# The recurrent stage of a four-block kernel: query sum in PSUM, gate inputs of 64 steps in a bank, exp sums by copies, one gate op per half

## The chip, the cores and the metric

The kernel runs on one core of one Trainium2 chip. A core has five engines that run their own instruction streams and meet through semaphores: TensorE (PE; weight loads are listed apart as PEld), VectorE (DVE), ScalarE (ACT), GpSimd (POOL) and SyncE (SP), which issues the DMAs. Matmuls write PSUM, whose banks hold 512 float32 values in each of 128 partitions. The metric is the device time of one execution in microseconds.

## The reference

A sequence `x` (2 batches, 512 positions, 128 channels) passes through four blocks, L0 to L3. Each adds two parts to it, a conditioned one (`xcond`) and a feed-forward one (`ffn`), each on a layer norm of `x`. All is float32. The change touches L1's `xcond` alone. That part is a recurrent cell (GRU) of 512 steps, which at each step attends over the 77 context vectors of its batch with the state as query:

```
def step(h, x_t):
    hid = broadcast(h[:, None, :], (B, 77, 128))
    combined = concatenate([hid, enc_hiddens], axis=2)
    score = tanh(einsum('bsk,kh->bsh', combined, W_att))
    score = einsum('bsh,h->bs', score, V_att[:, 0])
    attn = softmax(score, axis=-1)
    context = einsum('bs,bsh->bh', attn, enc_hiddens)
    inp = concatenate([x_t, context], axis=1)
    gz, gr, gh = split(inp @ Wi + b, 3, axis=1)
    rz, rr, rh = split(h @ Uh, 3, axis=1)
    z = sigmoid(gz + rz)
    r = sigmoid(gr + rr)
    hh = tanh(gh + r * rh)
    h_new = z * h + (1.0 - z) * hh
    return h_new, h_new
outs = scan(step, last_hidden, x_t of 512 positions)
```

`B` is 2, `h` has 128 channels, and `last_hidden` is the conditioning vector. No step can begin before the state of the step before it is there.

## The kernel before

The function `tile_kernel` runs eight phases one after the other, two for each block. Tensors are kept with 128 positions or 128 channels on the partitions. Weights come by DMA three phases ahead. The phase that matters is `l1_xcond` (lines 571 to 663). It keeps channels on the partitions, so that the state `h` of a step is a tile of 128 x 2, one column per batch, in `hs[:, s, :]`.

Ahead of the loop it prepares what does not depend on the state. `gx` holds for each of 512 positions eight columns: the input's share of the three gates for two batches (with the bias), and two columns of zeros. `stat` (128 x 2 x 77) is the context's share of the argument of the score's tanh. `gc` (128 x 2 x 3 x 77) is the product of each context vector with the three gates' weights, so that the context vector itself is never formed. `vrep` holds the score vector in all of its 128 columns: a matmul with it leaves the scores on every partition. `uhh` is half of the last third of `Uh`, since the sigmoids are computed as tanh of half the argument.

A step of the loop then does this, one line of the profile for each operation (matmuls go through the helper at line 222, and are told apart by the tiles that they write and read: `mm`, `tr` and `o` are PSUM tiles, of three, three and two banks):

- The query: `pu` (mm) is a matmul of `wtop` with `h`. L621, on VectorE and for each batch, adds its column to that batch's 77 columns of `stat` and writes `x`. L623 is the tanh on ScalarE (`th`). The matmul with `vrep` (tr) gives the scores.
- The state's share of the gates: a bank `pc` (o) holds eight columns. It was filled during the step before with `gx` of this step, by a matmul with the identity (`gates_in`). Three more matmuls add the state's share (`uh` twice, `uhh` once with `h` read twice), the first of them between the query and the scores, the others behind the scores.
- The softmax and the context's share: L631 takes the negated largest score of each batch (`nm`). L636 takes the exponential on ScalarE (`e`), and with `accum_out` its sum (`se`), which a second instruction reads out of an accumulator. L637 multiplies `gc` by `e` (`pr`, 231 columns per batch). L639 inverts the sums (`ri`), L641 reduces both batches of `pr` to six columns (`pre`), L642 multiplies them by `ri`, and L643 adds the six columns of `pc`.
- The gates: L645 is the tanh of the first two gates of both batches (`zr`). L648, one per batch, is the tanh of the candidate (`hh`), with its bias and scale read from `pre` and `zr`. L651, L653 and L654 form the two factors of the blend, and L656, one per batch, writes the new state's column into `hs`.

The loop stands inside `manual_schedule()`: each engine issues its instructions of the loop in the order in which the program states them. Which semaphores an instruction waits for is worked out by the framework from the tiles that it reads and writes.

Every float32 matmul here shows as two passes, each with a weight load and a matmul of its own, so a step has 14 of each.

## Time and profile before

| | us |
|---|---|
| median of 3 runs | 6283.16 (6280.9 to 6301.28) |
| the profiled execution's own time | 6284.0 |
| its span, first to last instruction | 6282.2 |
| PE, PEld, DVE, ACT, POOL busy | 4528.6, 3080.0, 3299.4, 2077.1, 227.0 |
| the loop of 512 steps | 258.6 to 3281.2 |
| mean granted TensorE clock | 0.665 |

Times are microseconds from the start of the span. An engine's busy time is that of its own instructions, without waits. A line of the costliest groups reads: source line, engine, operation, tiles written and read, shapes, count, then busy time, mean duration in ns, and idle time of the engine just ahead of the group with what ended most of it. The granted clock is the share of TensorE's full speed that it was given. The slices below cut the span in 40 equal parts, some 157 us each; a digit is the busy share (or the clock) in tenths:

```
PE   4855555555555555555559999798888888888888
DVE  6555555555555555555555443453636353545423
ACT  1333333333333333333333333132323232333322
PEclk7855555555555555555559998787969697878856
```

### The profile page before, as it was taken

Reading aid. Unit: us, or ns where it says so; the run is one execution under the profiler, and the core shown is the slowest. Engines: PE = TensorE matmul, PEld = TensorE weight load, DVE = VectorE, ACT = ScalarE, POOL = GpSimd, SP = SyncE. Lnnn points to the kernel's source line nnn. Section 1 sums busy time; section 2 is a strip of 40 time slices with the busy share of each in tenths; the row PEclk is TensorE's granted clock in tenths of the full one; section 3 lists DMA queues with packets and bytes.
Section 4 is the critical chain, followed back from the end, with each engine's and each line's share of the span. In section 5 each row is a group of like instructions: output and inputs, shape, how many; then the busy total and the mean of one; then the engine's idle time right before and its main releaser. Section 6 shows DMA issues by size and latency. Waiting matters only on the chain. (4 is left out here: it accounts for less than half of the span.)

```text
span 6282.2 us, 63201 instructions
## 1 busy us (share of the span) xinstructions
PE 4528.6 (72%) x21576; PEld 3080.0 (49%) x21576; DVE 3299.4 (53%) x10933; ACT 2077.1 (33%) x6069; POOL 227.0 (4%) x228
## 2 busy tenths in 40 slices
PE   4855555555555555555559999798888888888888
PEld 2655555555555555555555667534333333333356
DVE  6555555555555555555555443453636353545423
ACT  1333333333333333333333333132323232333322
POOL 2000000000000000000000000100000010101000
PEclk7855555555555555555559998787969697878856
DMA  1000000000000000000000000100000000000000
GB/s 37 26 1 1 0 1 1 1 1 1 1 1 1 1 1 1 1 1 1 1 15 21 1 1 4 37 1 2 10 1 12 1 12 1 13 1 1 1 0 4
DMA packets 6973, 32.96 MB, mean 5 GB/s; under 512 B 1872, under 2 KB 4202, under 8 KB 4986
## 3 DMA queue, kind: packets, MB, share of 16 engines
q1 hardware_dynamic: 6650, 28.93, 1.3%
q8 instruction: 170, 2.79, 0.2%
q14 instruction: 153, 1.25, 0.1%
HBM read 28.40 MB, written 0.52 MB: 5 GB/s over the span
## 5 line engine op out<-in xcount | busy, mean ns | idle before, releaser
L222 PE MATMUL mm<-hs,w1x 128*128 128x2 f32 x1024 | 300.2, 363 | 1203.8 <-DVE hs L656 1203.8
L222 PEld LDWEIGHTS mm<-hs,w1x 128*128 128x128 f32 x1024 | 256.2, 310 | 1252.1 <-DVE hs L656 1249.0
L1058 DVE TENSOR_REDUCE peak<-st 128x2 f32<-128x1024 f32 (+1 forms) x480 | 528.8, 1136 | 311.1 <-PE st L222 306.0
L222 PE MATMUL tr<-th,vrep 128*128 128x77 f32 x2048 | 580.5, 436 | 120.5 <-ACT th L623 120.5
L222 PE MATMUL st<-qx,km 32*128 32x512 f32 (+1 forms) x1920 | 533.1, 717 | 69.3 <-DVE peak L1058 62.5
L222 PEld LDWEIGHTS o<-hs,w1x 128*128 128x128 f32 x2048 | 559.3, 333 | 0.0
L222 PEld LDWEIGHTS tr<-th,vrep 128*128 128x128 f32 x2048 | 473.7, 321 | 164.5 <-ACT th L623 164.5
L222 PE MATMUL o<-hs,w1x 128*128 128x2 f32 x2048 | 549.7, 338 | 0.0
L631 DVE TENSOR_REDUCE nm<-tr 128x1 f32<-128x77 f32 x1024 | 243.4, 238 | 570.7 <-PE tr L222 570.7
L1159 ACT ACTIVATE pT<-st 128x1024 f32<-128x1024 f32 x384 | 388.5, 1023 | 430.2 <-PE st L222 429.4
L636 ACT ACTIVATE e<-tr,nm 128x77 f32<-128x77 f32 x1024 | 334.1, 326 | 463.9 <-DVE nm L631 458.0
L623 ACT ACTIVATE th<-x 128x77 f32<-128x77 f32 x1024 | 226.7, 268 | 654.3 <-DVE x L621 654.3
L222 PE MATMUL st<-km,qm 32*128 32x512 f32 (+1 forms) x3072 | 410.7, 541 | 41.5 <-DVE qm L1043 16.6
L637 DVE TENSOR_TENSOR pr<-gc,e 128x231 f32<-128x231 f32 x1024 | 409.7, 400 | 43.0 <-ACT e L636 0.8
L621 DVE TENSOR_SCALAR x<-stat,mm 128x77 f32<-128x77 f32 x1024 | 226.4, 264 | 358.9 <-PE mm L222 358.9
L645 ACT ACTIVATE zr<-pre 128x4 f32<-128x4 f32 x512 | 105.5, 206 | 823.3 <-DVE pre L643 823.3
L641 DVE TENSOR_REDUCE pre<-pr 128x6 f32<-128x462 f32 x512 | 324.7, 634 | 0.0
L222 PEld LDWEIGHTS st<-km,qm 32*128 32x128 f32 x3072 | 206.4, 247 | 212.5 <-issue 89.4
L648 ACT ACTIVATE hh<-o,pre,zr 128x1 f32<-128x1 f32 x1024 | 303.8, 347 | 17.8 <-ACT zr L645 0.2
L222 PEld LDWEIGHTS st<-qx,km 32*128 32x128 f32 (+1 forms) x1920 | 150.7, 192 | 319.4 <-DVE peak L1058 201.6
L222 PE MATMUL o<-gx,ident 128*128 128x8 f32 x1024 | 293.8, 361 | 0.0
L222 PE MATMUL o<-hs,uhh 128*128 128x4 f32 x1024 | 290.5, 354 | 0.0
(340 smaller groups left out, 6621.8 us busy)
## 6 DMA issues: line engine op xcount, KB each, us to landing
w3x<-in_w3x SPq DMA_DIRECT2D x6, 1664.0 KB, 7.3
w1g<-in_w1g SPq DMA_DIRECT2D x1, 2560.0 KB, 9.0
w2a<-in_w2a SPq DMA_DIRECT2D x1, 2176.0 KB, 8.5
w2b<-in_w2b SPq DMA_DIRECT2D x1, 2176.0 KB, 9.0
w3f<-in_w3f SPq DMA_DIRECT2D x1, 1940.0 KB
w0g<-in_w0g SPq DMA_DIRECT2D x1, 1760.0 KB, 12.7
w1d<-in_w1d SPq DMA_DIRECT2D x1, 1288.0 KB, 5.5
rows<-in_rows SPq DMA_DIRECT2D x1, 1108.5 KB, 8.4
```

What stands on the lines that cost most here:

```text
L222: pe.matmul(o, lhsT, rhs, start=start, stop=stop)
L621: dve.tensor_scalar(x, stat[:, b, :], pu[:, b : b + 1], None, ALU.add)
L623: act.activation(th, x, AF.Tanh)
L631: dve.reduce_max(nm[:, b : b + 1], pb[b], axis=AX.X, negate=True)
L636: act.activation(e[:, b, :], pb[b], AF.Exp, bias=nm[:, b : b + 1], accum_out=se[:, b : b + 1])
L637: dve.tensor_tensor(pr[:, b], gc[:, b], bcast(e[:, b, :], [P, 3, NC], 1), ALU.mult)
L641: dve.tensor_reduce(pre, pr, AX.X, ALU.add)
L645: act.activation(zr, pre[:, :, 0:2], AF.Tanh, scale=0.5)
L648: act.activation(hh[:, b : b + 1], pc[:, 6 + b : 7 + b], AF.Tanh, bias=pre[:, b, 2:3], scale=zr[:, b, 1:2])
L1058: dve.tensor_reduce(dst if dst.ndim == 2 else dst.rearrange("p t r -> p r t"), src, AX.X, ALU.max, negate=True)
L1159: act.activation(pT[:, 2 * p : 2 * p + 2, :], ps, AF.Exp)
```

## The change

All of it lies in `l1_xcond`.

- The sum of query and context is formed in PSUM. `states_in` fills 154 columns of a bank with `stat`, by a matmul with the identity, ahead of the step that uses it. In the step, one matmul per batch adds `wtop` times the state, with the batch's column of `h` read 77 times over (a stride-0 operand). The tanh reads PSUM. The two operations of L621 are gone.
- `gates_in` fills a whole bank, 512 columns, with `gx` of 64 steps at once. A step uses its eight columns of that bank. The first of the three matmuls that add the state's share moves behind the scores, to the two others.
- The exponential no longer sums. A copy of `e` on ScalarE, one per batch and behind both exponentials, has the `accum_out` instead.
- The reduction of `pr` stands ahead of the reciprocal and writes a tile of its own, `cg`. The product with `ri` and the sum with `pc` become one operation per batch.

```diff
+            SB = 64
             gx = r1.tile([P, S, 4, B], F32, tag="gx", name="gx")
...
             def gates_in(s):
 
-                pc = o_tile()[:, :8]
-                mm(pc, ident, gx[:, s].rearrange("p g b -> p (g b)"), start=True, stop=False)
-                return pc
+                bank = o_tile()
+                mm(bank, ident, gx[:, s : s + SB].rearrange("p s g b -> p (s g b)"))
+                return bank
+
+            def states_in():
+
+                xp = mm_tile()[:, :n2].rearrange("p (b n) -> p b n", b=B)
+                mm(xp, ident, stat)
+                return xp
+
+            def add(o, lhsT, rhs):
+                pe.matmul(o, lhsT, rhs, start=False, stop=True, skip_group_check=True)
 
             with tc.manual_schedule():
-                pc = gates_in(0)
+                bank, xp = gates_in(0), states_in()
                 for s in range(S):
                     h = hs[:, s, :]
-                    pu = mm_tile()[:, :B]
-                    mm(pu, w("wtop"), h)
-                    mm(pc[:, 0:2], w("uh")[:, :P], h, start=False, stop=False)
+                    pc = bank[:, 8 * (s % SB) : 8 * (s % SB) + 8]
                     pb = []
                     for b in range(B):
-                        x = rs.tile([P, NC], F32, tag="x", name="x")
-                        dve.tensor_scalar(x, stat[:, b, :], pu[:, b : b + 1], None, ALU.add)
+                        add(xp[:, b, :], w("wtop"), h[:, b : b + 1].to_broadcast([P, NC]))
+                    for b in range(B):
                         th = rs.tile([P, NC], F32, tag="th", name="th")
-                        act.activation(th, x, AF.Tanh)
+                        act.activation(th, xp[:, b, :], AF.Tanh)
                         t = tr_tile()[:, :NC]
                         mm(t, vrep, th)
                         pb.append(t)
-                    mm(pc[:, 2:4], w("uh")[:, P : 2 * P], h, start=False, stop=False)
-                    mm(pc[:, 4:8].rearrange("p (c b) -> p c b", b=B), uhh, bcast(h, [P, 2, B], 1), start=False, stop=True)
+                    for g in range(2):
+                        add(pc[:, 2 * g : 2 * g + 2], w("uh")[:, g * P : (g + 1) * P], h)
+                    add(pc[:, 4:8].rearrange("p (c b) -> p c b", b=B), uhh, bcast(h, [P, 2, B], 1))
+                    if s + 1 < S:
+                        xp = states_in()
...
                     for b in range(B):
-                        act.activation(e[:, b, :], pb[b], AF.Exp, bias=nm[:, b : b + 1], accum_out=se[:, b : b + 1])
+                        act.activation(e[:, b, :], pb[b], AF.Exp, bias=nm[:, b : b + 1])
                         dve.tensor_tensor(pr[:, b], gc[:, b], bcast(e[:, b, :], [P, 3, NC], 1), ALU.mult)
+                    for b in range(B):
+                        es = rs.tile([P, NC], F32, tag="es", name="es")
+                        act.activation(es, e[:, b, :], AF.Copy, accum_out=se[:, b : b + 1])
+                    cg = rs.tile([P, B, 3], F32, tag="cg", name="cg")
+                    dve.tensor_reduce(cg, pr, AX.X, ALU.add)
                     ri = rs.tile([P, B], F32, tag="ri", name="ri")
                     dve.reciprocal(ri, se)
                     pre = rs.tile([P, B, 3], F32, tag="pre", name="pre")
-                    dve.tensor_reduce(pre, pr, AX.X, ALU.add)
-                    dve.tensor_tensor(pre, pre, bcast(ri, [P, B, 3], 2), ALU.mult)
-                    dve.tensor_tensor(pre, pc[:, 0:6].rearrange("p (g b) -> p b g", b=B), pre, ALU.add)
+                    for b in range(B):
+                        dve.scalar_tensor_tensor(pre[:, b, :], cg[:, b, :], ri[:, b : b + 1], pc[:, b : 6 : B], ALU.mult, ALU.add)
...
-                    pcn = gates_in(s + 1) if s + 1 < S else None
+                    if (s + 1) % SB == 0 and s + 1 < S:
+                        bank = gates_in(s + 1)
...
-                    pc = pcn
```

## The prediction

> **What bounds it now.** I read the page's 40 slices first, then the costliest groups with what ended their idle time, then the timeline of one step, then the busy time by stretch. The slices show one flat stage from the third to the 21st: the recurrence, 512 dependent steps. The groups say that its engines wait for each other in a ring (TensorE for the state, written at L656).

> ```profile
> L222 PE MATMUL mm<-hs,w1x 128*128 128x2 f32 x1024 | 300.2, 363 | 1203.8 <-DVE hs L656 1203.8
> ...
> L623 ACT ACTIVATE th<-x 128x77 f32<-128x77 f32 x1024 | 226.7, 268 | 654.3 <-DVE x L621 654.3
> ```

> So no engine's sum counts, only the length of one turn. The timeline of a step (start, busy time, engine, line, names, shapes, count; "x2" is two merged):

> ```profile
> 2005.53 0.34 ACT L648 ACTIVATE hh<-o,pre,zr 128x1 f32<-128x1 f32 x1
> 2005.81 0.35 DVE L656 SCALAR_TENSOR_TENSOR hs<-hh,oz,zh 128x1 f32<-128x1 f32 x2
> 2006.21 0.50 PEld L222 LDWEIGHTS mm<-hs,w1x 128*128 128x128 f32 x2 [2.44 <-DVE hs L656]
> 2006.22 0.58 PE L222 MATMUL mm<-hs,w1x 128*128 128x2 f32 x2 [2.35 <-DVE hs L656]
> ...
> 2006.84 0.44 DVE L621 TENSOR_SCALAR x<-stat,mm 128x77 f32<-128x77 f32 x2 [0.68 <-PE mm L222]
> 2007.14 0.44 ACT L623 ACTIVATE th<-x 128x77 f32<-128x77 f32 x2 [1.27 <-DVE x L621]
> ...
> 2007.46 1.14 PE L222 MATMUL tr<-th,vrep 128*128 128x77 f32 x4 [0.23 <-ACT th L623]
> ...
> 2008.64 0.24 DVE L631 TENSOR_REDUCE nm<-tr 128x1 f32<-128x77 f32 x1 [0.19 <-PE tr L222]
> ...
> 2008.91 0.33 ACT L636 ACTIVATE e<-tr,nm 128x77 f32<-128x77 f32 x1
> 2008.93 0.83 DVE L637 TENSOR_TENSOR pr<-gc,e 128x231 f32<-128x231 f32 x2
> ...
> 2009.13 0.19 ACT L636 ACTIVATION_READ_ACCUMULATOR e<-tr,nm 128x1 f32 x1
> ...
> 2009.67 0.16 DVE L639 RECIPROCAL ri<-se 128x2 f32<-128x2 f32 x1
> 2009.79 0.63 DVE L641 TENSOR_REDUCE pre<-pr 128x6 f32<-128x462 f32 x1
> 2010.46 0.17 DVE L642 TENSOR_TENSOR pre<-pre,ri 128x6 f32<-128x6 f32 x1
> 2010.73 0.17 DVE L643 TENSOR_TENSOR pre<-o,pre 128x6 f32<-128x6 f32 x1
> 2010.93 0.21 ACT L645 ACTIVATE zr<-pre 128x4 f32<-128x4 f32 x1 [1.61 <-DVE pre L643]
> ...
> 2011.71 0.35 DVE L656 SCALAR_TENSOR_TENSOR hs<-hh,oz,zh 128x1 f32<-128x1 f32 x2
> ```

> The reader should see a turn of 5.90 us (2005.81 to 2011.71; 5.893 unrounded, times 512 = 3017 us, near half the span) and that a small thing hides in it: the first hs starts at 2005.81, before the second hh ends at 2005.87. A read of one column of an SBUF tile waits for that column's write alone.

> **Before, with 2005.81 as zero:** both hs written 0.35; query weights load 0.40; both passes end 0.99; x 1.03; th 1.33; tr 1.65; second nm 2.83; second e 3.10; its accumulator read 3.32 to 3.51; second pr (0.83 less one pr of 0.40 after 3.12) 3.55 to 3.95, thus released by that accumulator read; reduce 3.98; product 4.65; sum 4.92; zr 5.12; hs 5.90.

> **Query sum in PSUM.** It removes two x (L621) and makes the 2-column matmul into two of 77 columns, one per batch, onto a bank that the identity has filled with stat in the step before. Gain at the front: the first add reads only column 0 of h, so by the hh/hs row it need not wait for the second hs. One hs takes 0.22 (mean of L656 in the groups by form), so its weights load at 0.27, not 0.40. The second add comes two passes later, after the second hs. Cost: both adds stand ahead of both th in program order and write one bank. Does the first th wait for the second add? The nearest row is in the fourth block, where four matmuls (eight passes) fill one bank and ACT reads it quarter by quarter:

> ```profile
> 4084.55 1.05 PE L222 MATMUL o<-w3x,YT 128*128 128x128 f32 x8
> ...
> 4085.77 1.15 ACT L1141 ACTIVATE va<-o,keep 128x128 f32<-128x128 f32 x4 [27.46 <-PE o L222]
> ```

> The first quarter is read at 4085.77, 0.17 after the eighth pass ends (4085.60), though its own two passes were done about 0.7 earlier. PSUM is guarded by the whole bank, unlike SBUF. So the first th waits for all four passes, and behind it on ACT the other th and both e, and tr on TensorE: 1.14 by the tr row of the same shape, which puts their end at 0.27 + 1.14 = 1.41.

> [...]

> Then th starts 0.04 later (as x after mm), 1.45. It now reads PSUM and has no bias or scale from memory. No row has this at 77 columns: from above the SBUF th, 0.27; from below the PSUM copy of 512 columns (L1072, 0.585), whose 0.83 ns a column leaves 0.16 + 77 x 0.83 ns = 0.22. I take 0.24, nearer the PSUM row: 1.69. tr follows after 0.05 (as th to tr now) at 1.74, the second nm 1.18 later (2007.46 to 2008.64) at 2.92, against 2.83. The x is gone, but waiting for the other batch costs more than it and the head start bring.

> A stride-0 operand of 77 columns is in no row. Below: no gain is possible, since weight loads set the pass rate (77-column passes come 0.21 apart, as 2-column ones do). Above: columns read at half rate (0.50 for a first pass of 77 against 0.37 for 2, so 1.7 ns a column, 0.13 more, and three gaps of 0.26 in place of 0.21) would cost 0.26 a step, 133 us. The nearest row, uhh with its doubled h, takes 0.354 against 0.352 for two columns, so I take nothing.

> The identity matmul on stat (154 columns, two passes of at most 0.26), the four uh passes and two uhh passes follow tr. uhh ends near 4.05, needed at 4.79: cover 0.74. The identity ends near 4.6, needed by 6.2.

> **Exp sums by copies.** Without the sum, e no longer ends with an accumulator read on DVE's path: second e 2.92 + 0.27 = 3.19, ends 3.52, second pr 3.55 to 3.95, reduce 3.98. These are the times of before, so the 0.09 lost ahead of nm comes back here. The copies (about 0.27 each by the SBUF th) and their reads (0.19) queue on ACT behind the second e: 3.42 + 4 pieces, about 0.8, done near 4.2, and only ri waits for them, at 4.53: 0.3 of cover, and nothing else of ACT is due before zr. If the cover were gone, each 0.1 beyond it costs 51 us. A table reload is not expected: Copy stands among Exp in the fourth block (L1072 beside L1159) with one load a layer.

> **One gate op per half.** The reduce goes first, then ri, then two three-element ops in place of product and sum. Four ops as before, but ri now lies behind the reduce. From 3.98: reduce ends 4.61; ri, independent of it, starts 0.08 before that end, as it does now before the end of pr (2009.67 against 2009.76): 4.53 to 4.69; the first op after 0.10 (L642 to L643 now: a two-semaphore wait, TensorE and DVE itself; again so); 4.79; the second 0.14 later, as the two hs; ends 5.14; zr 5.17. Before: 5.12. Bounds: one semaphore alone would save 0.07 (reduce to product takes 0.03), 35 us; no overlap of ri costs 0.08, 43 us. From zr to hs nothing changes (0.78): 5.95.

> **Gate inputs of 64 steps.** The per-step identity (two passes, off the path, 2009.19) goes; seven times in the loop two passes of 512 columns come instead, 0.85 apart in the third block (four in 3.6 us at clock 0.50 from 4028.4). They run from 4.4 to 6.1, in TensorE's idle stretch, and cost at most 0.3 each, 2 us. Worth nothing: what it replaces was hidden.

> **Sum.** 5.944 against 5.893 unrounded, +0.05 a step, 512 steps: +26 us, less 2 for seven brief chances of a faster clock. The profiled execution took 6284.0 (span 6282.2), the median is 6283.16, so both move to about 6308. About 0.3% (19 us) is what the measurement can tell from no change. My own range, by the bounds above without the stride-0 one: 6265 to 6365.

> **Clock.** The granted clock is 0.50 through the stage, at 56% busy (stretch and length, busy time and count of matmuls, loads, DVE, ACT, POOL, then clock, DMA share, GB/s):

> ```profile
> 400.00:1000.00 600.00, 337.73 (x1428) 319.39 (x1428) 352.34 (x1524) 210.92 (x917) 0.00 (x0) 0.50 0.00 1
> ```

> It rises elsewhere after 3.4 us full of 512-column passes (4028.4 to 4031.8 at 0.50, the next 3.4 us at 1.00), some 2000 columns. The new step has at most about 650 columns in any 3.4 us, so I leave it at 0.50. [...]

> **Rivals.** First, not slower: the th of a batch waits for its own add alone. Then th starts at 0.27 + 0.71 + 0.04, the second tr at 1.74 and the second nm 0.42 before my forecast: -0.37 a step, 6283 - 189 = 6094. It decides as soon as the bank is guarded by column; the va rows speak against it. 17%. Second, slower: the stretched operand makes the first add wait for the whole h. +0.13 a step on my sum: 6308 + 66 = 6374. Against it hh and hs. 12%. Third, the clock rises: the first step, run partly at 1.00, has four tr passes in 0.84 in place of 1.14, so 0.30 each on adds and tr: 6308 - 307, about 6000. 4%. Fourth, no change: the first gate op waits for one semaphore alone, 6308 - 35 = 6273. For it, nothing but that the wait before is a detail of how semaphores were shared out; against it, its two inputs, pc from TensorE and ri. 12%. My forecast: 55%.

> The range, 6240 to 6385, leaves out the first and third (21%). Chances: faster 0.26 (first, third and a tail), same 0.19, slower 0.55.

> **What would show it.** Right: th released by TensorE 1.1 to 1.2 after the first add's weights load; that load after the first hs; second nm near 2.9; second pr released by e; ri just ahead of the reduce's end; clock 0.50. Wrong: th about 0.75 after that load; ri waiting for ACT; the first op of the gates right behind ri; a clock above 0.5.

## The result, and the profile after

| | before | after |
|---|---|---|
| median of 20 runs beside each other | 6273.99 | 6297.15 |
| span of the profiled execution | 6282.2 | 6295.2 |
| loop, from the first state written to the last | 3016.6 | 3039.3 |
| median step (first `hs` to first `hs`) | 5.895 | 5.942 |
| after the loop | 3001.4 | 2989.6 |

The ratio is 1.0028, 95% interval 1.0015 to 1.0041: 9 to 26 us slower. The medians lie 23.2 us apart, more than the 17.6 of the ratio, which weighs every execution: six of the 20 before lay 22 us or more above their median, and two of the 20 after. The loop's times are worked out from the traces, over all 512 steps. It grew by 22.7 us in the two profiles; the span grew by 13.0 only, because the 3000 us behind the loop, whose instructions are the same, were 11.8 us shorter in this execution.

The costliest groups of the page after, which correspond to the two shown of before. L619 is now the line of the additive matmuls, L631 the tanh.

```profile
L619 PE MATMUL mm<-hs,w1x 128*128 128x77 f32 x2048 | 581.2, 438 | 745.3 <-DVE hs L672 745.3
...
L631 ACT ACTIVATE th<-mm 128x77 f32<-128x77 f32 x1024 | 185.6, 234 | 713.4 <-PE mm L619 713.4
```

The tanh is released by TensorE. It waits longer in all (713 us, not 654), although VectorE's addition between them is gone. One step of the timeline after:

```profile
2003.32 0.35 DVE L672 SCALAR_TENSOR_TENSOR hs<-hh,oz,zh 128x1 f32<-128x1 f32 x2
2003.59 0.93 PEld L619 LDWEIGHTS mm<-hs,w1x 128*128 128x128 f32 x4 [2.19 <-DVE hs L672]
2003.59 1.14 PE L619 MATMUL mm<-hs,w1x 128*128 128x77 f32 x4 [1.81 <-DVE hs L672]
2004.76 0.36 ACT L631 ACTIVATE th<-mm 128x77 f32<-128x77 f32 x2 [1.39 <-PE mm L619]
...
2005.05 1.14 PE L222 MATMUL tr<-th,vrep 128*128 128x77 f32 x4 [0.33 <-ACT th L631]
...
2006.22 0.24 DVE L642 TENSOR_REDUCE nm<-tr 128x1 f32<-128x77 f32 x1 [0.19 <-PE tr L222]
2006.43 0.82 DVE L648 TENSOR_TENSOR pr<-gc,e 128x231 f32<-128x231 f32 x2
...
2007.12 0.19 ACT L651 ACTIVATION_READ_ACCUMULATOR es<-e 128x1 f32 x1
...
2007.28 0.63 DVE L653 TENSOR_REDUCE cg<-pr 128x6 f32<-128x462 f32 x1
2007.84 0.16 DVE L655 RECIPROCAL ri<-se 128x2 f32<-128x2 f32 x1
2008.10 0.34 DVE L658 SCALAR_TENSOR_TENSOR pre<-cg,ri,o 128x3 f32<-128x3 f32 x2
2008.47 0.21 ACT L660 ACTIVATE zr<-pre 128x4 f32<-128x4 f32 x1 [1.16 <-DVE pre L658]
...
2009.25 0.35 DVE L672 SCALAR_TENSOR_TENSOR hs<-hh,oz,zh 128x1 f32<-128x1 f32 x2
```

Read it from the first `hs`. The weights load 0.27 later, while the second `hs` is still being written (until 0.35). The four additive passes end at 1.41, and only then does the first tanh start, at 1.44. The second `nm` is at 2.90 where it was at 2.83; `pr` follows it by 0.21 where it was 0.29; and behind the reduction the gates take 1.19 (2007.28 to 2008.47) where they took 1.14.

### The profile page after: what moved, and what is told of

Read it like the earlier page. It is cut to its first block, busy times and chain, and to the rows that moved or that the text cites. A ratio compares the mean times of both kernels' runs of the same rounds, so it can differ in the third digit from the quotient of the medians.

```text
span 6295.2 us, 65280 instructions
## 1 busy us (share of the span) xinstructions
PE 4952.8 (79%) x22616; PEld 3295.6 (52%) x22616; DVE 3078.0 (49%) x9909; ACT 2196.7 (35%) x7093; POOL 227.1 (4%) x228
## 3 DMA queue, kind: packets, MB, share of 16 engines
q8 instruction: 178, 2.92, 0.2%
## 5 line engine op out<-in xcount | busy, mean ns | idle before, releaser
L619 PE MATMUL mm<-hs,w1x 128*128 128x77 f32 x2048 | 581.2, 438 | 745.3 <-DVE hs L672 745.3
L619 PEld LDWEIGHTS mm<-hs,w1x 128*128 128x128 f32 x2048 | 474.9, 323 | 946.0 <-DVE hs L672 946.0
L642 DVE TENSOR_REDUCE nm<-tr 128x1 f32<-128x77 f32 x1024 | 242.9, 237 | 1201.9 <-PE tr L222 1201.9
L222 PE MATMUL tr<-th,vrep 128*128 128x77 f32 x2048 | 580.8, 438 | 167.2 <-ACT th L631 167.2
L222 PEld LDWEIGHTS tr<-th,vrep 128*128 128x128 f32 x2048 | 474.3, 322 | 273.8 <-ACT th L631 273.8
L222 PE MATMUL st<-qx,km 32*128 32x512 f32 (+1 forms) x1920 | 529.5, 710 | 69.2 <-DVE peak L1073 62.5
L619 PEld LDWEIGHTS o<-hs,w1x 128*128 128x128 f32 x2048 | 496.4, 332 | 0.0
L619 PE MATMUL o<-hs,w1x 128*128 128x2 f32 x2048 | 477.2, 337 | 0.0
L222 PE MATMUL st<-km,qm 32*128 32x512 f32 (+1 forms) x3072 | 408.0, 538 | 41.4 <-DVE qm L1058 16.5
L222 PE MATMUL mm<-stat,ident 128*128 128x154 f32 x1024 | 438.8, 532 | 0.0
L631 ACT ACTIVATE th<-mm 128x77 f32<-128x77 f32 x1024 | 185.6, 234 | 713.4 <-PE mm L619 713.4
L648 DVE TENSOR_TENSOR pr<-gc,e 128x231 f32<-128x231 f32 x1024 | 408.8, 400 | 15.2 <-ACT e L647 1.3
L653 DVE TENSOR_REDUCE cg<-pr 128x6 f32<-128x462 f32 x512 | 324.4, 634 | 17.6
L222 PEld LDWEIGHTS st<-qx,km 32*128 32x128 f32 (+1 forms) x1920 | 150.1, 191 | 319.9 <-DVE peak L1073 202.3
L222 PEld LDWEIGHTS st<-km,qm 32*128 32x128 f32 x3072 | 203.9, 244 | 212.0 <-issue 89.0
L619 PE MATMUL o<-hs,uhh 128*128 128x4 f32 x1024 | 289.8, 353 | 0.0
L222 PEld LDWEIGHTS mm<-stat,ident 128*128 128x128 f32 x1024 | 278.6, 332 | 0.5 <-ACT gc L604 0.2
```

The costliest lines, as they stand in the source:

```text
L222: pe.matmul(o, lhsT, rhs, start=start, stop=stop)
L619: pe.matmul(o, lhsT, rhs, start=False, stop=True, skip_group_check=True)
L631: act.activation(th, xp[:, b, :], AF.Tanh)
L642: dve.reduce_max(nm[:, b : b + 1], pb[b], axis=AX.X, negate=True)
L648: dve.tensor_tensor(pr[:, b], gc[:, b], bcast(e[:, b, :], [P, 3, NC], 1), ALU.mult)
L653: dve.tensor_reduce(cg, pr, AX.X, ALU.add)
```

## Experiments

The theory is the prediction's: the sum in PSUM loses about 0.09 a step because the tanh of one batch waits for the other batch's add in the same bank, the copies give 0.09 back, and the gate operations lose 0.05. Median steps below are worked out from each trace; ratios are to the kernel before, with 95% intervals.

**The parts alone.** `sum_only` undoes the copies and the gate operations:

```diff
-                        act.activation(e[:, b, :], pb[b], AF.Exp, bias=nm[:, b : b + 1])
+                        act.activation(e[:, b, :], pb[b], AF.Exp, bias=nm[:, b : b + 1], accum_out=se[:, b : b + 1])
...
-                    dve.tensor_reduce(cg, pr, AX.X, ALU.add)
...
+                    dve.tensor_reduce(pre, pr, AX.X, ALU.add)
+                    dve.tensor_tensor(pre, pre, bcast(ri, [P, B, 3], 2), ALU.mult)
+                    dve.tensor_tensor(pre, pc[:, 0:6].rearrange("p (g b) -> p b g", b=B), pre, ALU.add)
```

> Leaves in the query sum in PSUM and the bank of 64 steps; the exp sums, the reduction, the product and the sum are as before. Theory (the first tanh waits for both adds): the second nm comes 0.09 later in a step than before and nothing gives it back, so a step of about 5.98 us against 5.895, +43 us, ratio to the kernel before 1.007. Rival (the loss is in the gate operations behind the softmax, the sum in PSUM is neutral): a step of 5.89, ratio 1.000.

Measured: 1.0063 [1.0046, 1.0081], step 5.976. `soft_only` is the other half: these lines in their changed form, on the kernel before.

> The kernel before with only the exp sums by copies, the reduction ahead of the reciprocal and one gate operation per half. Theory: the second pr starts 0.09 earlier, the gate operations take 0.055 longer, so a step of about 5.86 against 5.895, -18 us, ratio 0.997. Rival (this part makes the loss): a step of 5.94, ratio 1.004 or more.

Measured: 0.9970 [0.9956, 0.9984], step 5.855. Timeline of `sum_only`, then of `soft_only`:

```profile
2001.72 0.35 DVE L668 SCALAR_TENSOR_TENSOR hs<-hh,oz,zh 128x1 f32<-128x1 f32 x2
...
2004.63 0.24 DVE L642 TENSOR_REDUCE nm<-tr 128x1 f32<-128x77 f32 x1 [0.19 <-PE tr L222]
...
2004.92 0.83 DVE L648 TENSOR_TENSOR pr<-gc,e 128x231 f32<-128x231 f32 x2
```

```profile
2002.23 0.35 DVE L660 SCALAR_TENSOR_TENSOR hs<-hh,oz,zh 128x1 f32<-128x1 f32 x2
...
2005.05 0.24 DVE L631 TENSOR_REDUCE nm<-tr 128x1 f32<-128x77 f32 x1 [0.19 <-PE tr L222]
...
2005.26 0.83 DVE L637 TENSOR_TENSOR pr<-gc,e 128x231 f32<-128x231 f32 x2
```

With the sum alone the second `nm` is late (2.91) and `pr` follows by the old 0.29. With the softmax part alone it is on time (2.82) and `pr` follows by 0.21. The two differences, +0.081 and -0.040, add to the +0.047 of the whole within 0.006. The softmax part was worth having; the query sum undid it.

**Why the tanh is late.** `two_banks` gives each batch its own bank:

```diff
-                xp = mm_tile()[:, :n2].rearrange("p (b n) -> p b n", b=B)
-                mm(xp, ident, stat)
+                xp = [mm_tile()[:, :NC] for b in range(B)]
+                for b in range(B):
+                    mm(xp[b], ident, stat[:, b, :])
                 return xp
```

> The changed kernel with a bank of its own for each batch's query sum, filled by two identity matmuls. Theory: the first tanh then waits for its own two passes alone, the second tr starts right behind, the second nm comes 0.43 earlier than in the changed kernel: a step of about 5.52 us, some -190 us against before, ratio 0.970. Rival (the tanh is late for another reason than the shared bank, as the semaphore or a slow read of PSUM): within 0.05 of the changed kernel's 5.94, ratio 1.003.

Measured: 0.9689 [0.9649, 0.9728], step 5.513. Its timeline:

```profile
2006.79 0.35 DVE L673 SCALAR_TENSOR_TENSOR hs<-hh,oz,zh 128x1 f32<-128x1 f32 x2
2007.07 1.14 PE L620 MATMUL mm<-hs,w1x 128*128 128x77 f32 x4 [1.21 <-DVE hs L673]
2007.82 0.24 ACT L632 ACTIVATE th<-mm 128x77 f32<-128x77 f32 x1 [0.97 <-PE mm L620]
2008.11 1.14 PE L222 MATMUL tr<-th,vrep 128*128 128x77 f32 x4
2008.24 0.24 ACT L632 ACTIVATE th<-mm 128x77 f32<-128x77 f32 x1 [0.19 <-PE mm L620]
```

The same four passes of 1.14 run and the tanh still reads PSUM, but it starts 0.75 after they begin, in the middle of them. The cause is the shared bank. In this kernel the refills of 64 steps are no longer hidden: the steps at 64, 128, 256 and 384 take 5.72 to 5.73, 0.21 more, and those at 192, 320 and 448 take 5.56, 5.46 and 5.44.

`guard_order` asks whether the guard also holds in the other direction, against a write behind a read. Both score matmuls are put behind, so that TensorE's own order is not in the way:

```diff
                         add(xp[:, b, :], w("wtop"), h[:, b : b + 1].to_broadcast([P, NC]))
-                    for b in range(B):
                         th = rs.tile([P, NC], F32, tag="th", name="th")
                         act.activation(th, xp[:, b, :], AF.Tanh)
+                        ths.append(th)
+                    for th in ths:
                         t = tr_tile()[:, :NC]
                         mm(t, vrep, th)
```

> The changed kernel with each batch's tanh stated behind its own add, in the same bank, and both score matmuls behind the second add (so that TensorE's own order holds nothing up, as it did when the score matmul stood between the adds). Theory (the whole bank is guarded): the second add waits until the first tanh has read, though its columns are others; its weights load at 1.31 in the step, the second nm comes 0.18 later than in the changed kernel: a step of 6.12 us, ratio 1.034 of 5.94. Rival (guarded by columns): the first tanh overlaps the second add, the step of two banks, 5.51.

Measured: 1.0182 [1.0166, 1.0197], step 6.121. (The ratio in the text is a slip: 6.12 against 5.895, 512 times, is 1.018.) Its timeline:

```profile
2006.41 0.71 PE L619 MATMUL mm<-hs,w1x 128*128 128x77 f32 x2 [1.47 <-DVE hs L673]
2007.16 0.24 ACT L630 ACTIVATE th<-mm 128x77 f32<-128x77 f32 x1 [0.97 <-PE mm L619]
2007.45 0.71 PE L619 MATMUL mm<-hs,w1x 128*128 128x77 f32 x2 [0.33 <-ACT th L630]
```

The second add waits for ScalarE, which reads the other batch's columns: add, read, add, one after the other. The bank, not the column, is what is guarded here, both ways: in the changed kernel the first tanh starts at 1.44, after the second add (ended at 1.41), and in this run the second add starts 0.05 after the first tanh ends (2007.45 against 2007.40). The guard shows as a wait on a semaphore: in the trace after, the first L631 of a step waits for one of TensorE's. Each PSUM tile of this loop is 128 x 512, a whole bank, so no run here tells a guard by bank from a guard by tile; but it differs from the SBUF tile `hs`, where one column is waited for alone (the weights load at 0.27, with the second column written until 0.35). What happens without the guard no run here shows.

`between` was meant to show the same and didn't:

```diff
                         add(xp[:, b, :], w("wtop"), h[:, b : b + 1].to_broadcast([P, NC]))
-                    for b in range(B):
                         th = rs.tile([P, NC], F32, tag="th", name="th")
```

> The changed kernel with each batch's tanh and score matmul stated right behind its own add, in the same bank. Theory (the whole bank is guarded, against reads too): the second add now waits for the first tanh to have read, its four passes and the second tanh follow in a row, the second nm comes some 0.18 later than in the changed kernel: a step of 6.12 us, ratio 1.018. Rival (guarded by columns): the second add does not wait, and the step is that of two banks, 5.51, ratio 0.969.

Measured: 1.0525 [1.0476, 1.0575], step 6.545. Here the first score matmul stands between the adds in TensorE's order, and it waits for the first tanh; the second add is queued behind it whatever the guard. That is 0.6 (6.545 against 5.942) lost to the order of one engine, which the expectation overlooked, and it says nothing on the bank.

**Passes or columns.** `one_add` adds both batches by one matmul:

```diff
-                    for b in range(B):
-                        add(xp[:, b, :], w("wtop"), h[:, b : b + 1].to_broadcast([P, NC]))
+                    add(xp, w("wtop"), bcast(h, [P, B, NC], 2))
```

> The changed kernel with both batches added by one matmul of 154 columns in one bank, two passes in place of four. Theory: passes cost more than columns; the weights load at 0.40 in the step (both columns of the state), two passes end 0.86 later at 1.27 in place of 1.41, so a step of about 5.80, -50 us against before, ratio 0.992. Rival (columns with a stride-0 operand are what costs): no gain on the changed kernel or a loss, since the head start of the first hs is given up: 5.94 to 6.07, ratio 1.003 to 1.014.

Measured: 0.9930 [0.9908, 0.9952], step 5.814. Its timeline has the one matmul:

```profile
2001.38 0.35 DVE L671 SCALAR_TENSOR_TENSOR hs<-hh,oz,zh 128x1 f32<-128x1 f32 x2
2001.78 0.88 PE L619 MATMUL mm<-hs,w1x 128*128 128x154 f32 x2 [1.59 <-DVE hs L671]
```

Two passes of 154 columns are busy for 0.88, four of 77 for 1.14. That outweighs the lost head start of 0.13: as long as the tanh waits for both batches anyway, one matmul is the better way to write it (5.814 a step against 5.942).

**The head start.** `late_h` writes the second batch's column first:

```diff
-                    for b in range(B):
+                    for b in (1, 0):
                         dve.scalar_tensor_tensor(hs[:, s + 1, b : b + 1], hh[:, b : b + 1], oz[:, b : b + 1], zh[:, b : b + 1], ALU.mult, ALU.add)
```

> The changed kernel with the two state columns written in the other order, so that the first add, which reads column 0, waits for the last one written. Theory (a read of one column waits for that column alone, which gives a head start of 0.13): a step of 6.07 to 6.08 us against 5.94, ratio to the kernel before 1.014. Rival (the load of the query weights waits for the whole state in both orders): 5.94, ratio 1.003.

Measured: 1.0195 [1.0148, 1.0242], step 6.159, so 0.217 more than the changed kernel and not 0.13. The timeline shows where the other 0.08 went:

```profile
2003.95 0.59 ACT L663 ACTIVATE hh<-o,pre,zr 128x1 f32<-128x1 f32 x2
...
2004.23 0.16 DVE L670 TENSOR_TENSOR zh<-zh,hs 128x2 f32<-128x2 f32 x1
2004.58 0.35 DVE L672 SCALAR_TENSOR_TENSOR hs<-hh,oz,zh 128x1 f32<-128x1 f32 x2 [0.19 <-ACT hh L663]
2004.98 0.29 PEld L619 LDWEIGHTS mm<-hs,w1x 128*128 128x128 f32 x1 [2.06 <-DVE hs L672]
```

The first `hs` written now needs the second `hh`, which ends at 2004.54, so it starts 0.35 after the last `zh` began and not 0.26. The head start itself is there: the weights load 0.40 after the first `hs` and not 0.27, which is 0.13 of the 0.217.

**The refills.** `step_gates` fills eight columns for each step again:

```diff
-            SB = 64
+            SB = 1
...
-                mm(bank, ident, gx[:, s : s + SB].rearrange("p s g b -> p (s g b)"))
+                mm(bank[:, :8], ident, gx[:, s : s + SB].rearrange("p s g b -> p (s g b)"))
```

> The changed kernel with the gate inputs filled for each step alone, eight columns in two passes, in place of 64 steps at once. Theory (both are hidden): the median step stays 5.94, the three short bursts of a full clock at steps 128, 256 and 384 vanish (about 1 us in all), ratio to the kernel before 1.003 to 1.005. Rival (the bank of 64 steps is worth something of its own): 5.95 or more in every step.

Measured: 1.0055 [1.0036, 1.0075], step 5.940, no step below 5.93. The three short steps of the changed kernel (5.56 at 128, 256 and 384) are gone, and the loop takes 3039.7 where it took 3039.3: the refill is hidden. The ratio came 0.0005 above what was expected, and its interval overlaps that of the changed kernel.

**What the clock is worth.** The windows of the changed kernel at step 128 (stretch and length, then busy time and count of matmuls, loads, DVE, ACT, POOL, then clock):

```profile
1020.00:1023.40 3.40, 3.40 (x9) 1.88 (x9) 1.80 (x10) 0.86 (x4) 0.00 (x0) 0.50 0.00 0
1023.40:1026.80 3.40, 1.66 (x13) 1.41 (x12) 2.22 (x8) 1.42 (x9) 0.00 (x0) 1.00 0.00 0
1026.80:1030.00 3.20, 1.84 (x7) 1.63 (x8) 0.75 (x5) 1.15 (x5) 0.00 (x0) 0.50 0.01 3
```

After 3.4 us in which TensorE never rested (the refill and the next adds lay in it) came 3.4 us at full clock. To see what a step would be at that clock, `fill1`, `fill2` and `fill2_5` add work that TensorE does in its idle stretch and nobody reads, on top of two banks. `fill2_5`:

```diff
                         xp = states_in()
+                    fill = tr_tile()
+                    for k in (64, 64, 32):
+                        mm(fill[:, : 8 * k], ident, gx[:, 0:k].rearrange("p s g b -> p (s g b)"))
```

`fill1` and `fill2` have one and two matmuls of 512 columns there.

> The two-bank kernel with one more matmul of 512 columns per step in TensorE's idle stretch, its result not read. What the clock is worth: if the granted clock stays at 0.50, two passes of 0.85 end about 0.5 past the next step's start, a step of 5.8 to 6.1 us, ratio above 0.985. If 1024 columns more in a step raise the clock, adds and tr each lose 0.3: a step near 4.95, ratio near 0.92; a clock that comes and goes gives something between.

Measured: 0.9626 [0.9569, 0.9684]; the steps alternate between 4.87, some 5.5 and 5.73, the mean clock from 400 to 2800 us is 0.63.

> The same with two such matmuls per step. At a clock of 0.50 the four passes of 0.85 would push the next step out to some 7.7 us, ratio near 1.15; with the clock raised throughout, they end in time and the step is near 4.95, ratio near 0.92.

Measured: 0.9380 [0.9314, 0.9447]; median step 4.872, but every third to fifth near 5.74; clock 0.91.

> The two-bank kernel with two matmuls of 512 columns and one of 256 per step whose results are not read. If more columns keep the clock at 1.00 throughout, every step is 4.87 as the median of the run with two, ratio 0.921. If the drops come from where the busy stretch ends in the clock's window and not from the number of columns, it stays near 0.91 and 5.1 us, ratio 0.935; if the third matmul reaches past the next state, 0.2 is lost on every step, ratio 0.94 or more.

Measured: 0.9186 [0.9172, 0.9199]; median step 4.871, clock 0.99: the fastest kernel of the study. `before_fill2` adds two matmuls of 512 columns to the kernel before, behind `gates_in`:

> The kernel before with two matmuls of 512 columns per step whose results are not read. If the clock is what such a step waits for most, it rises to about 0.9 here too; the query's two passes lose 0.2 and the scores' four 0.29, so 5.40 us in most steps, about 5.5 in the mean, ratio 0.965. If it stays at 0.50, the four added passes of 0.85 push the next step out: 7.5 us, ratio 1.13.

Measured: 1.0701 [1.0664, 1.0739], step 6.793. The clock stayed near 0.50, as in the second case of the expectation, but only what the filling reaches past the next state is lost, 0.90 a step and not 1.6. A stretch of 1000 us in `fill2_5`, and the same in `before_fill2`:

```profile
1000.00:2000.00 1000.00, 954.18 (x4901) 644.64 (x4900) 606.48 (x2650) 470.04 (x2244) 0.00 (x0) 0.99 0.00 1
```

```profile
1000.00:2000.00 1000.00, 960.18 (x2670) 644.46 (x2668) 513.41 (x2222) 306.99 (x1334) 0.00 (x0) 0.51 0.00 1
```

TensorE is busy 95% and 96%, at clocks of 0.99 and 0.51. The busy share does not tell the clock. What a stretch must hold for the clock to rise can be estimated from the traces.

Inside each trace of the fourteen kernels, every stretch at one clock lasts a whole multiple of 3.413 us, such as the 3.4 and the 6.8 us of the bursts. In the traces before and after, all of these stretches start on one grid of that step, to 0.01 us.

Cut into windows of 3.413 us, the fourteen loops give 12230. The columns that TensorE streamed in each are an estimate: every pass's columns are spread evenly over the time between the end of the pass before and its own end. None of the 10504 windows below 1470 columns was followed by full clock, and all of the 1438 above 1660 were; in between both happened (138 to half clock, 150 to full). Busy time doesn't sort them: 1055 windows at half clock in which TensorE never rested, with up to 1535 columns, were followed by half clock again. `before_fill2` streams 1212 columns in a mean window, `fill2_5` 2445. In `before_fill2` the clock rose for 6.8 us once in some 250 us; its step of 6.79 is nearly two windows (6.83), so the windows meet almost the same part of the step for many steps. The count of columns fits all the traces, but no run varied it alone.

## Why the prediction was right

The mechanism, its place and its sizes held term by term (us after the first `hs`; measured in the step shown, to 0.01):

| | predicted | measured |
|---|---|---|
| first add's weights load | 0.27 | 0.27 |
| four additive passes end | 1.41 | 1.41 |
| first th | 1.45 | 1.44 |
| first tr | 1.74 | 1.73 |
| second nm | 2.92 | 2.90 |
| reduction | 3.98 | 3.96 |
| ri | 4.53 | 4.52 |
| first gate operation | 4.79 | 4.78 |
| zr | 5.17 | 5.15 |
| next hs (median step) | 5.944 | 5.942 |

- Query sum in PSUM: the head start was there (`late_h`), the wait on the whole bank too (`two_banks`, `guard_order`). Alone it cost 0.081 a step. The tanh took 0.234, in the lower part of the bounds. The stretched operand cost nothing: its four passes take 1.14, as those of `tr` do.
- Exp sums by copies: the second `pr` was released without the accumulator read. The copies ended 0.5 ahead of ri (2007.31 against 2007.84), more than the 0.3 worked out, because a copy and its read overlap (the first copy takes 0.26, its read starts 0.15 after the copy's start): the four pieces took 0.59. (One after another they come to 0.92 by the prediction's own figures and not to its 0.8, which would have left a cover of 0.2.)
- Gate operations: ri started 0.08 (median) ahead of the reduction's end and the first operation kept its two-semaphore wait (0.10 from the end of ri), so the fourth rival fell.
- Gate inputs: hidden, as said. Of seven chances of a faster clock three came true, 0.38 each, 1.1 us in all in place of 2.
- Clock: 0.50 but for those bursts. The third rival, a faster clock, fell. No run shows that a window in which TensorE never rests is enough for it: 1055 of them were followed by half clock. The prediction's reading by columns held, though fewer than its 2000 suffice: by the estimate above the windows ahead of the three bursts hold some 1640, all others at most 1274. The price of the third rival was nearly right: at full clock the step of two banks is 0.64 shorter (5.513 to 4.871), where 0.60 was worked out for adds and scores.
- First rival: fell as a forecast, but its time is what `two_banks` measured, 5.513 where 5.52 follows from it (189 us less worked out; 187 measured, 6084.70 against 6272.06). Second rival: fell, since the load comes 0.27 after the first `hs`.

The total held as well: 25 us were forecast, the medians lie 23.2 apart, and the loop of the two profiles grew by 22.7, which is explained (0.047 a step, 24 us, less the bursts). The 6308 came out as 6297.15 because the median before was 6273.99 in this comparison and not 6283.16.

The sum took the part behind the loop as unchanged. Its instructions are, but its time differed by 11.8 us between the two profiles, and its mean clock of 0.82 in both hides why. These are the same passes late in the fourth block, first before, then after:

```profile
5968.30:6007.00 38.70, 35.19 (x155) 12.84 (x150) 8.43 (x22) 10.21 (x12) 0.00 (x0) 0.50 0.00 0
5990.50:6016.50 26.00, 21.32 (x153) 8.23 (x150) 8.69 (x23) 10.09 (x12) 0.00 (x0) 0.95 0.00 1
```

At a clock of 0.50 they took 12.7 us longer than at 0.95; a few shorter stretches add to this and take from it. Over the fourteen kernels that part took between 2990 and 3043 us. In `fill2`, where it took 3041, a stretch earlier in it ran for 75 us at 0.50 for which the changed kernel needed 39 at 1.00. So a difference of 10 or 40 us in one profile need not come from the edit. Why the clock stays low in one execution and rises in another was not tried.

## What to carry to other kernels

A step that waits for everything in turn is read as one chain: an operation removed there is worth its time less what takes its place as the last thing to end. Here a PSUM bank shared by two halves made each half wait for the other, which cost 0.43 a step (5.942 against 5.513). Where both a matmul and a read are on the path, try a PSUM bank for each half, or one matmul that writes both (5.814). And where a small step leaves TensorE at half clock, look at the clock before the instructions: it was worth more here than any edit of the chain (5.513 to 4.871), though filling of the same kind made the kernel before slower (5.895 to 6.793).
